# A graph layer on one core: the order of the end rewritten, and the row products done part by part

## The chip, the core and the metric

The kernel runs on one core of one Trainium2 chip. The core has five engines that run their own instruction streams beside each other: TensorE (PE; its weight loads are shown apart, as PEld), VectorE (DVE), ScalarE (ACT), GpSimd (POOL) and SyncE (SP). SP, ACT and POOL also issue DMA transfers. The metric is the device time of one execution in microseconds (us), smaller is better. It was 2201.93 us before the change, the median of 3 runs (2199.54 to 2204.43).

## The reference

There are N = 12500 nodes with 128 features and E = 212500 edges, sorted by destination, with 128 features and a weight each. The layer has 8 heads of 16 features. Cut to what matters:

```python
h = relu(layernorm(x))
q, v = h @ Wq.T + bq, h @ Wv.T + bv          # per node
k    = edge_attr @ Wk.T + bk                 # per edge
logits = sum16(q[src]*k), sum16(q[dst]*k), sum16(q[src]*q[dst])   # 3 x 8 per edge
score  = (softmax_by_dst(l0/4) + softmax_by_dst(l1/4) + softmax_by_dst(l2/4)) * weight**lam
out    = segment_sum(score[..., None] * v[dst], dst) @ Wo.T + bo
return x + leaky_relu(out, 0.1)
```

`softmax_by_dst` takes a maximum, an exponential and a sum over all edges with the same destination. As `v[dst]` is the same for all edges of a node, the sum over edges is a sum of scores per node and head, and the product with `v` is done once per node.

## The kernel before, in words

Edges are cut into blocks of 512 (`BE`), and the list into S = 5 parts of 83 blocks each. A turn t handles block t of all five parts; there are G = 83 full turns (0 to 82) and a short one, t = G = 83, which holds what is left over: the last 20 edges and the heads of the following parts. Below, g = 5t + s counts blocks.

In the main loop each block goes through PE, ACT and DVE. `turn` transposes the edge features, `project` makes k (`k_ps`), `spread_q` makes q of the destination (`qd_ps`), POOL gathers q of the sources (`gather`, line 702), and `logits` (lines 1250 to 1253, DVE) multiplies and sums by head. Per turn, with the five parts side by side in 120 rows (5 x 24 logits), there follow:

- `turn_logits` (PE, `l_ps`), `turn_head` (PE, `h_ps`) and `scan_here`, `scan_head`, `scan_on` (DVE, `u`, `u_head`, `head`): running maxima along the edges;
- `scan_back` (DVE, `m`): the same backwards, which gives each edge its node's maximum;
- `turn_max` (PE, `m_ps`), `powers` (DVE subtracts, ACT takes the exponential; tile `back`), `weigh_powers` (DVE, times the edge's weight);
- `show_ends` (PE `d_ps`, ACT; tile `sel`): a 0/1 matrix that says which of 42 (`W`) consecutive nodes an edge belongs to;
- `to_rows` (PE `w_ps`, line 1403; ACT copies to `rows`, line 1408): the sums per node, as products of `sel` and `back`;
- `put_rows` (SP, line 1419): five DMAs per turn that write each part's 42 rows to `sums[s]` in memory, at a node that is known only at run time. `fetch` loads these node numbers into registers (line 665).

Before the change `to_rows` multiplies three parts by three parts at once and keeps the diagonal blocks:

```python
trios = [(0, (0, 1, 2)), (S - 3, (1, 2))]      # 126 columns of sel by 144 of back, 2 x 4 products
```

Nodes are finished in units of 256, two units at a time (class `Nodes`): `load_sums`, `scores` (`scores_of`, lines 1112 to 1118: add, clamp, reciprocal, multiply, add, add), `turn` (PE and an ACT copy), `project_v`, `weigh` (DVE, line 1178), `turn`, `project_o` (PE, then a scaled ACT copy, line 1189), `add_x` (DVE, lines 1194 and 1195), `store` (SP). Most pairs do this inside the loop. What is left for the end is the last pair (`last_pair`, units 8 and 47) and `rest`: five groups of units, [18, 9], [10, 19], [28, 29], [38, 39] and [48]. Seven of these nine units lie across two parts, so a second transfer (issued by ACT, into `more`) and an add (line 1732) complete their sums. Each group of `rest` holds its product with Wv in a PSUM bank (`hold`).

The order on each engine is written out by hand: `pin` chains every instruction to the one pinned before it on the same engine, so an engine takes its instructions in the order of the source lines. [...] PSUM tiles made by `small` share three buffers. The end, from the line `leaving, last_pair = ...` on, is one such written order. The register load of line 665 was not pinned.

## Time and profile before

| | us |
|---|---|
| median of 3 runs | 2201.93 (2199.54 to 2204.43) |
| the profiled execution | 2203.34 |
| its span | 2201.5 |
| DVE busy | 2050.1 (93%) |
| PE busy | 1779.5 (81%) |
| POOL busy | 1586.5 (72%) |
| ACT busy | 1372.0 (62%) |
| last gather leaves POOL | 2131.2 |
| last `logits` of the loop on DVE ends | 2137.9 |

How to read the rows. A row of a timeline gives the start in us from the begin of the span, the busy time, the engine, the line, the operation, the tiles (written <- read), the shapes, how many instructions were merged (x16), and in brackets how long the engine stood before it and what released it. A row of the page gives a group's busy time and mean ns, then the idle time before its instructions. A row of waits gives the sum, the number of times and the longest. A row of windows gives the busy time of PE, PEld, DVE, ACT and POOL in that stretch, then the granted PE clock (1.00 is full) and the DMA share. One fp32 product of PE shows as two records, a transpose as one. Names with q (SPq, ACTq) are the engine's queue, here DMA issues and register loads.

### The profile page before, as it was taken

The numbers are of one execution on the slowest core, as the hardware profiler recorded it, in microseconds if no ns is written. First come the engines' busy times: TensorE is split into PE (matmuls) and PEld (weight loads), VectorE is DVE, ScalarE is ACT, GpSimd is POOL, SyncE is SP. The second block draws the span as 40 slices with busy tenths as digits, with TensorE's granted clock in tenths as the row PEclk, the third lists the DMA queues.
The fourth block names the chain that finished last, engine by engine and source line by source line (L and its number), as shares of the span: only waits on it lengthen the run. The fifth ranks groups of instructions, "written<-read, shape, count | busy, mean of one in ns | idle before, by whom it ended". The sixth has DMA issues, their size and how long they took to land.

```text
span 2201.5 us, 36690 instructions
## 1 busy us (share of the span) xinstructions
PE 1779.5 (81%) x10812; PEld 1418.5 (64%) x10812; DVE 2050.1 (93%) x2893; ACT 1372.0 (62%) x2555; POOL 1586.5 (72%) x1676
## 2 busy tenths in 40 slices
PE   4677888877887888888888888888888978888785
PEld 2565766666666666666766766766666767666664
DVE  6877999999999999999999999999999999999994
ACT  4777656665666566666656666666666656666671
POOL 7746777777777777777777777777777777777750
PEclk8788778787788778877878787787878787787887
DMA  8585456556646555655555565565555555555531
GB/s 227 168 252 159 145 150 181 158 162 177 169 148 189 165 161 154 187 162 164 157 169 154 144 186 149 156 171 151 151 167 162 154 170 155 150 171 158 156 99 58
DMA packets 373744, 355.66 MB, mean 162 GB/s; under 512 B 187698, under 2 KB 293437, under 8 KB 373327
## 3 DMA queue, kind: packets, MB, share of 16 engines
q1 hardware_dynamic: 304493, 237.91, 37.1%
q0 software_dynamic: 53184, 108.92, 17.8%
q10 hardware_dynamic: 15856, 6.39, 1.2%
q8 instruction: 87, 1.43, 0.3%
q14 instruction: 124, 1.02, 0.2%
HBM read 320.83 MB, written 32.17 MB: 160 GB/s over the span
## 4 chain that ended last, share of the span: by engine, by line
DVE 50%; PE 14%; DMA 11%; issue 4%; ACT 3%; POOL 1%; DVEq 1%; SPq 0%; ACTq 0%; POOLq 0%
DVE lT L1253 18%; DMA qq<-q_table,sources 11%; DVE prod L1250 7%; DVE prod L1252 7%; DVE prod L1251 7%; DVE m L1343 4%; PE k_ps L1231 4%; DVE l_ps L1313 3%; PE w_ps L1403 2%; PE eT_ps L1222 2%; DVE back L1363 1%; POOL qq L702 1%; PE m_ps L1355 1%; PE k_ps L1229 1%; DVE back L1375 1%
## 5 line engine op out<-in xcount | busy, mean ns | idle before, releaser
L702 POOL DMA_INDIRECT qq<-q_table,sources x1580 | 1498.2, 948 | 520.1 <-issue 219.1
L1253 DVE TENSOR_REDUCE lT<-prod 128x96 f32<-128x1536 f32 x415 | 727.4, 1753 | 14.3
L1231 PEld LDWEIGHTS k_ps<-wk,eT 128*128 128x128 f32 x3320 | 505.6, 233 | 201.2 <-issue 199.9
L1231 PE MATMUL k_ps<-wk,eT 128*128 128x128 f32 x3320 | 597.2, 335 | 0.7 <-ACT eT L1224 0.7
L1242 ACT COPY qd<-qd_ps 128x512 f32<-128x512 f32 x415 | 244.4, 589 | 138.7 <-DVE prod L1252 133.3
L1222 PE MATMUL eT_ps<-ident,ea 128*128 128x128 f32 x1660 | 310.3, 319 | 18.5 <-ACT eT L1224 16.1
L1364 ACT ACTIVATE back<-back 128x480 f32<-128x480 f32 x83 | 50.1, 604 | 416.8 <-DVE back L1363 416.8
L693 ACT ACTIVATE relb<-relb,before 126x512 bf16<-126x512 bf16 x415 | 303.4, 731 | 0.0
L1250 DVE TENSOR_TENSOR prod<-qq,qd_ps 128x512 f32<-128x512 f32 x412 | 279.0, 677 | 14.6 <-ACT qd L1242 9.1
L1239 PE MATMUL qd_ps<-win,oh 126*128 126x128 bf16 x1660 | 189.5, 245 | 124.2 <-DVE prod L1250 95.4
L1252 DVE TENSOR_TENSOR prod<-qd,k_ps 128x512 f32<-128x512 f32 x415 | 281.7, 679 | 0.0
L1251 DVE TENSOR_TENSOR prod<-qq,k_ps 128x512 f32<-128x512 f32 x412 | 279.7, 679 | 0.0
L1224 ACT COPY eT<-eT_ps 128x512 f32<-128x512 f32 x415 | 239.7, 578 | 62.6 <-PE eT_ps L1222 53.6
L1222 PEld LDWEIGHTS eT_ps<-ident,ea 128*128 128x128 f32 x1660 | 232.6, 165 | 60.0 <-ACT eT L1224 41.6
L694 ACT ACTIVATE oh<-relb 126x512 bf16<-126x512 bf16 x415 | 261.4, 630 | 13.2
L1239 PEld LDWEIGHTS <-oh 126*128 126x128 bf16 x1660 | 151.9, 112 | 148.2 <-issue 138.2
L1229 PE MATMUL k_ps<-b,ones 3*128 3x512 bf16 x415 | 186.7, 450 | 73.0 <-DVE prod L1252 70.9
L1403 PE MATMUL w_ps<-back,sel 128*126 128x144 f32 (+1 forms) x1344 | 212.6, 319 | 28.0 <-ACT sel L1393 12.6
L1403 PEld LDWEIGHTS w_ps<-back,sel 128*126 128x126 f32 (+1 forms) x1344 | 202.3, 219 | 34.4 <-ACT sel L1393 15.8
L1355 PE MATMUL m_ps<-ident,m 120*128 120x120 f32 x332 | 83.4, 400 | 85.4 <-DVE m L1343 80.8
L1355 PEld LDWEIGHTS m_ps<-ident,m 120*128 120x128 f32 x332 | 56.4, 217 | 104.1 <-DVE m L1343 67.4
L1343 DVE TENSOR_TENSOR_SCAN m<-far,head,l_ps 120x512 f32<-120x512 bf16 x81 | 102.9, 1271 | 0.0
(222 smaller groups left out, 1770.1 us busy)
## 6 DMA issues: line engine op xcount, KB each, us to landing
ea<-in_edge_attr_dram SPq DMA_DIRECT2D x83, 1280.0 KB
relb<-rel_d SPq DMA_DIRECT2D x83, 630.0 KB
qq<-q_table,sources POOLq DMA_INDIRECT x1580
win<-q_table SPq DMA_DIRECT2D x415, 31.5 KB
far<-far_d SPq DMA_DIRECT2D x84, 120.2 KB
q_table<-q SPq DMA_DIRECT2D x24, 384.0 KB
sums<-rows SPq DMA_DIRECT2D x412, 7.9 KB
q_table<-xq SPq DMA_DIRECT2D x24, 256.0 KB
```

Of the source, the lines that this page charges most:

```text
L693: pin(nc.scalar.activation(d, d, AF.Abs, bias=before[:K3]))
L694: pin(nc.scalar.activation(oh, d, AF.Relu, bias=1.0, scale=-1.0))
L702: rows = pin(nc.gpsimd.indirect_dma_start(out=qq[:, j, :], out_offset=None, in_=x if g < RAW else q_table, in_offset=bass.IndirectOffsetOn ...
L1222: pin(nc.tensor.transpose(eT_ps[:, j, :], eas[g // S][:, g % S, j * F:(j + 1) * F], ident))
L1231: pin(nc.tensor.matmul(k_ps[:, j, :], eTs[g][:, j, :], wk, start=False, stop=(j == JN - 1)))
L1239: pin(nc.tensor.matmul(qd_ps[:, j, :], ohs[g][:, j * P:(j + 1) * P], d["win"][:, s, :], start=(j == 0), stop=(j == JN - 1)))
L1242: pin(nc.scalar.copy(qds[g], qd_ps))
L1250: pin(nc.vector.tensor_mul(prod[:, :, 1, :], qqs[g], q_ps[g]))
L1251: pin(nc.vector.tensor_mul(prod[:, :, 0, :], qqs[g], ks[g]))
L1252: pin(nc.vector.tensor_mul(prod[:, :, 2, :], qds[g], ks[g]))
L1253: pin(nc.vector.tensor_reduce(lTs[t][:, :, s, :], prod.rearrange("p j i (h d) -> p j (i h) d", d=DIM), AX.X, ALU.add))
L1403: pin(nc.tensor.matmul(w_ps[:, i].rearrange("p s c -> p (s c)"), d["sel"][:n, j, lo:lo + 3, :].rearrange("p s w -> p (s w)"), d["back"][:n ...
```

## The change

Five things change.

1. **Row products by part.** `to_rows` makes one product per part and column group, 42 columns of `sel` by 48 of `back`: 20 products where there were 8. `w_ps` and `rows` have 42 rows of 5 x 48; `rows` has three buffers. This holds for all 84 turns. The tile `back` of the short turn becomes two tiles from the pool of x, in two halves, with two exponentials and two weighings.
2. **The order of the end.** `show_ends` of the turns G-1 and G, which stood in the last step of the loop, is spread over the end; `turn_logits(G-1)` comes first; scans, `turn_max`, `powers`, `weigh_powers`, `to_rows` and `put_rows` of the last three turns are interleaved turn by turn; the last pair's `scores` and `weigh` come after them.
3. **Two queues for the last rows.** The short turn's five row DMAs are issued by ACT. The node numbers of that turn are loaded into registers of SP and of ACT, and both loads are pinned at their place in the loop (turn G-2, step 3).
4. **Neighbouring units.** `rest` becomes [9, 10], [18, 19], [28, 29], [38, 39] and [48]; the sums of a group come with one transfer per part (`load_last`): five on SP, then four on ACT.
5. **Scores pair by pair.** Each group adds its second part (the first on DVE, the other three on POOL), computes its own scores, weighs, turns and projects (into the bank it held) before the next group begins; `add_x` and `store` follow two groups later.

```diff
-        _, base_v[t] = nc.values_load_multi_w_load_instructions(
-            places[0:1, t, 0:S], engines=[mybir.EngineType.SP], min_val=0, max_val=N - 1,
+        to = [mybir.EngineType.SP] if t < G else [mybir.EngineType.SP, mybir.EngineType.Activation]
+        loads, base_v[t] = nc.values_load_multi_w_load_instructions(
+            places[0:1, t, 0:S], engines=to, min_val=0, max_val=N - 1,
...
+        if t == G:
+            for inst in loads:
+                pin(inst)
...
+        def load_last(self, to, q, which):
+            of = [u for u in self.of if len(parts_of(u)) > which]
+            if of:
+                s, i = parts_of(of[0])[which], self.of.index(of[0])
...
+                pin(q.dma_start(
+                    to[:, 2 * i:2 * (i + len(of))].rearrange("p (u k) i c -> p u (k i c)", k=2),
+                    sums[s][of[0] * UN:(of[0] + len(of)) * UN].rearrange(
+                        "(u p k) i c -> p u (k i c)", p=P, k=2)))
...
-    rest = [Nodes(rest[i:i + 2]) for i in range(0, len(rest), 2)]
+    rest, left = [], sorted([u for _, u in todo] + [u for u in range(NU) if stored_at(u) is None])
+    while left:
+        n = 2 if len(left) > 1 and left[1] == left[0] + 1 else 1
+        rest.append(Nodes(left[:n]))
+        left = left[n:]
+    rest.sort(key=lambda of: -of.n)
...
-            w_ps = small([3 * W, 2, 3, 2 * H3], "w_ps")
-            for i, (lo, _) in enumerate(trios):
+            w_ps = small([W, S, 2 * H3], "w_ps")
+            for s in range(S):
                 for j in range(JN):
...
+                    pin(nc.tensor.matmul(w_ps[:, s, :], d["sel"][:n, j, s, :],
+                                         d["back"][j][:n, s].rearrange("p i c -> p (i c)"),
+                                         start=(s == 0 and j == 0), stop=(s == S - 1 and j == JN - 1)))
-            rows = work.tile([3 * W, 2, 3, 2 * H3], F32, name="rows")
+            rows = work.tile([W, S, 2 * H3], F32, name="rows", bufs=3)
...
-                    for i in (G - 2, G - 1, G):
-                        show_ends(i)
+                    show_ends(G - 2)
...
-        leaving.store()
-        put_rows(G - 3, range(1, S))
         turn_logits(G - 1)
-        last_pair.scores()
         last_pair.turn(small([P, JN, P], "node_ps"))
+        show_ends(G - 1)
+        leaving.store()
+        put_rows(G - 3, range(1, S))
         scan_on(G - 1)
-        hold(rest[0], "eT_ps")
-        last_pair.project_v(ps.tile([P, JN, F], F32, name="k_ps", bufs=2))
         scan_back(G - 2)
         turn_max(G - 2)
         scan_on(G)
         scan_back(G - 1)
+        powers(G - 2)
+        last_pair.project_v(ps.tile([P, JN, F], F32, name="k_ps", bufs=2))
+        scan_back(G)
         turn_max(G - 1)
-        scan_back(G)
+        weigh_powers(G - 2)
+        show_ends(G)
         turn_max(G)
-        for t in (G - 2, G - 1, G):
-            powers(t)
-        for t in (G - 2, G - 1, G):
-            weigh_powers(t)
+        powers(G - 1)
+        to_rows(G - 2)
+        put_rows(G - 2)
+        powers(G)
+        weigh_powers(G - 1)
+        to_rows(G - 1)
+        put_rows(G - 1)
+        weigh_powers(G)
+        to_rows(G)
+        put_rows(G, q=nc.scalar)
+        last_pair.scores()
         last_pair.weigh(last_pair.held)
-        for t in (G - 2, G - 1, G):
-            to_rows(t)
-            put_rows(t)
-        for r, of in enumerate(rest):
-            of.load_sums(ends_ab[:, r * JN:r * JN + of.n], of.more)
-        for r, name in ((1, "k_ps"), (2, "qd_ps"), (3, "qd_ps"), (4, "k_ps")):
-            hold(rest[r], name)
         last_pair.turn(small([P, JN, P], "node_ps"))
+        hold(rest[0], "eT_ps")
         last_pair.project_o(small([P, JN, F], "node_ps"))
+        for which, q in ((0, nc.sync), (1, nc.scalar)):
+            for r, of in enumerate(rest):
+                of.load_last(ends_ab[:, r * JN:r * JN + of.n] if which == 0 else of.more, q, which)
+        for of, name in zip(rest[1:], ("k_ps", "qd_ps", "qd_ps", "k_ps")):
+            hold(of, name)
         last_pair.add_x(nc.vector)
         last_pair.store()
-        ab = ends_ab[:, :sum(of.n for of in rest)]
+        score = scan.tile([P, len(rest) * JN, HEADS], F32, name="end_score", bufs=1)
         for r, of in enumerate(rest):
+            ab = ends_ab[:, r * JN:r * JN + of.n]
             if of.more is not None:
-                some = ends_ab[:, r * JN:r * JN + of.n]
-                pin(nc.vector.tensor_add(some, some, of.more))
-        score = scan.tile([P, len(rest) * JN, HEADS], F32, name="end_score", bufs=1)
-        scores_of(ab, score[:, :ab.shape[1]])
-        for r, of in enumerate(rest):
-            of.score = score[:, r * JN:(r + 1) * JN]
+                pin((nc.vector if r == 0 else nc.gpsimd).tensor_add(ab, ab, of.more))
         for r in range(len(rest) + 2):
             if r < len(rest):
-                rest[r].weigh(rest[r].held)
-            if 0 <= r - 1 < len(rest):
-                rest[r - 1].turn(small([P, JN, P], "node_ps"))
+                of = rest[r]
+                of.score = score[:, r * JN:(r + 1) * JN]
+                scores_of(ends_ab[:, r * JN:r * JN + of.n], of.score[:, :of.n])
+                of.weigh(of.held)
+                of.turn(small([P, JN, P], "node_ps"))
+                of.project_o(of.held)
             if 0 <= r - 2:
-                rest[r - 2].project_o(small([P, JN, F], "node_ps"))
                 rest[r - 2].add_x(nc.vector)
                 rest[r - 2].store()
```

58 lines of the change are left out of this document (27 added, 31 removed).

## The prediction

> **What bounds the kernel now.** I read the page first, then the waits and the timeline of the loop, then the timelines of the five engines and the chain of waits from 2131 us to the end. The page says that VectorE (DVE) is busy nearly always and GpSimd (POOL) issues one row gather after another; TensorE (PE) has room.
>
> ```profile
> span 2201.5 us, 36690 instructions
> PE 1779.5 (81%) x10812; PEld 1418.5 (64%) x10812; DVE 2050.1 (93%) x2893; ACT 1372.0 (62%) x2555; POOL 1586.5 (72%) x1676
> L702 POOL DMA_INDIRECT qq<-q_table,sources x1580 | 1498.2, 948 | 520.1 <-issue 219.1
> ```
>
> 1580 gathers at 0.948 us, with 0.3 us between (520.1 / 1580 = 0.33), are about 2020 us of issue in a row: a floor for the loop that no part of the change touches. DVE meets that floor only at the very end: the last gather leaves POOL at 2131.2 and its products start 3 us later, which is a landing (2.4 us, row below) and little more.
>
> ```profile
> 2130.28 0.95 POOL L702 DMA_INDIRECT qq<-q_table,sources  x1 [0.30 <-issue]
> 2134.21 0.68 DVE L1250 TENSOR_TENSOR prod<-qq,qd_ps 128x512 f32<-128x512 f32 x1
> DVE u_head L1321 <- PE h_ps L1281: 2.9, 2, 2.2
> 202.50 0.58 PE L1281 MATMUL h_ps<-ident,lT 16*120 16x16 f32 x4
> 203.12 0.35 DVE L1321 TENSOR_TENSOR_SCAN u_head<-far,carry,h_ps 120x64 f32<-120x64 bf16 x1 [0.70 <-PE h_ps L1281]
> 2116.13 0.40 PE L1281 MATMUL h_ps<-ident,lT 16*120 16x16 f32 x4
> 2118.92 0.35 DVE L1321 TENSOR_TENSOR_SCAN u_head<-far,carry,h_ps 120x64 f32<-120x64 bf16 x1
> ```
>
> These pairs (first and last of 81) show where PE stands nearest to DVE in a turn: `h_ps` follows the row products of `to_rows` on PE, and DVE's `u_head` needs it. I took the distance from the end of the one to the start of the other for all 81: it is 0.04 us in the first pair and 2.4 in the last; 2 are below 0.5 us, 6 below 1.0, 20 below 1.5, 30 below 2.0. What `to_rows` grows by eats from that.
>
> The end of the kernel is 64 us in which no engine is full. Rows of the timeline, of ACT's waits and of the chain, in order of time:
>
> ```profile
> 2134.44 3.01 PE L1403 MATMUL w_ps<-back,sel 128*126 128x144 f32 x16 [2.29 <-DVE back L1375]
> 2137.38 2.17 PE L1389 MATMUL d_ps<-shows,ends_t 21*128 21x420 bf16 x4
> 2141.24 1.11 PE L1273 MATMUL l_ps<-ident,lT 128*120 128x128 f32 x4
> 2142.38 1.28 DVE L1331 TENSOR_TENSOR_SCAN u<-far,u,l_ps 120x512 f32<-120x512 bf16 x1 [1.14 <-PE l_ps L1273]
> 2147.11 0.20 DVE L1348 TENSOR_TENSOR m_end<-head,l_end 120x64 f32<-120x64 f32 x1
> 2151.31 6.31 PE L1403 MATMUL w_ps<-back,sel 128*126 128x144 f32 x48 [1.19 <-DVE back L1375]
> ACT back L1368 <- PE w_ps L1403: 2.5, 1, 2.5
> ACT rows L1408 <- DMA sums<-rows: 2.2, 1, 2.2
> 2154.41 8.77 SPq L1419 DMA_DIRECT2D sums<-rows  x15
> 2159.53 1.34 SPq L665
> 2162.91 4.03 ACTq L1145 DMA_DIRECT2D qq<-sums  x7
> 2163.28 5.75 SPq L1143 DMA_DIRECT2D ends_ab<-sums  x9
> 2164.63 2.36 DMA qq<-sums
> ACT hT L1165 <- DMA qq<-sums: 8.4, 1, 8.4
> 2170.35 0.70 DVE L1194 TENSOR_TENSOR node_ps<-h,node_ps 128x512 f32<-128x512 f32 x1 [14.97 <-ACT h L1189]
> 2171.69 1.95 DVE L1732 TENSOR_TENSOR ends_ab<-ends_ab,qq 128x384 f32<-128x384 f32 x4
> 2179.40 0.69 DVE L1178 TENSOR_TENSOR qq<-eT_ps,end_score 128x512 f32<-128x512 f32 x1
> 2194.41 0.42 DVE L1195 TENSOR_TENSOR qq<-node_ps,qq 128x256 f32<-128x256 f32 x1
> ```
>
> To be seen: DVE stands 15 us before 2170.35, while SP puts out fifteen row blocks (with a register load of 1.34 us among them) and both queues issue sixteen loads; then 7.7 us (2171.69 to 2179.40) of sums and scores for all the last units before the first of them goes on.
>
> **The change, part by part.** I lay the new order along the clock with these durations. Turns are G-2 = 81, G-1 = 82, G = 83.
>
> *Before the scans.* Of three `show_ends` only that of 81 stays ahead of `turn_logits`: after `w_ps` (2137.5, taken as long as before, see below) two `d_ps` at 0.55 and `l_ps` at 1.1 end at 2139.7. The scan starts at 2139.75, not 2142.38: 2.6 earlier. The scores of the pair that DVE did in that gap move to where it waits for PE and ACT, at no cost as long as it does wait.
>
> *Scans to row products.* Six scans took 4.9 us (2142.38 to 2147.3); with the subtraction for 81 among them `weigh_powers(81)` ends at about 2146.2. But PE gets there later: behind the `m_ps` of 81 (2143.8) now stand `project_v` of the last pair, `m_ps` of 82, `show_ends(83)` and `m_ps` of 83.
>
> ```profile
> 2145.74 0.60 PE L1168 MATMUL k_ps<-b,ones 3*128 3x512 bf16 x1
> 2146.27 2.08 PE L1170 MATMUL k_ps<-wv,hT 128*128 128x128 f32 x8
> 2146.00:2149.00 3.00, 3.00 (x14) 2.73 (x14) 1.31 (x2) 0.00 (x0) 0.00 (x0) 0.50 0.00 0
> ```
>
> That is 2.5 + 0.9 + 1.1 + 0.4: the products of 81 start at 2148.45 (2151.31 before, 2.9 earlier). ACT must take the two new `d_ps` and the 0.9 us rectifier ahead of the exponential of 82; that one ends at about 2150, its weights at 2150.6, still before PE is through with 81. The window (PE, weight loads, DVE, ACT and POOL busy, then the granted clock) shows 0.50 although PE was busy all 3.00 us of it; I keep that. [...]
>
> *Row products by part.* 20 products of 42 columns by 48 in place of 8 of 126 by 144: 40 records for 16, in each of 84 turns.
>
> ```profile
> 2061.71 2.23 PE L1403 MATMUL w_ps<-back,sel 128*126 128x144 f32 x16 [1.23 <-ACT sel L1393]
> 2061.71 2.01 PEld L1403 LDWEIGHTS w_ps<-back,sel 128*126 128x126 f32 x16 [1.42 <-ACT sel L1393]
> L1281 PE MATMUL h_ps<-ident,lT x328: 202/205/278, 162.7 to 2116.3; 16*120 16x16 f32 x164
> ```
>
> No row has this shape. Low end: by streamed columns, 20 x 48 against 8 x 144, 0.83 of 2.23 = 1.9 us. The nearest small product is `h_ps`: four in 0.40 us, one 0.205, so (0.40 - 0.205) / 3 = 0.065 us a step; 40 steps are 2.6 + 0.2 = 2.8 us, 0.6 more than now. High end: nothing of the loading hidden, `h_ps`'s 0.065 plus a load at the 0.05 that 42 of 126 columns of a 0.13 us load (2.01 / 16) make, 0.1 us or more: 4.2 us, 2.0 more. I take 2.8, since `h_ps` loads 120 columns at that pace and these load 42. At the lowered clock 16 records cost 3.0 us (2134.44), and by columns 40 cost no more. In the loop +0.6 on PE meets the distances above: the sum of what lies below 0.6 us is about 1.1 us in all; DVE waits for the last gathers anyway, so I take +0.5 for the whole loop. ACT's copy of the rows shrinks a little (240 columns for 288), hidden.
>
> *Rows out.* Three products at 2.8 end at 2151.2, 2154.0 and 2156.8 (before: all at 2157.5). A third `rows` buffer and a `back` of its own for 83 remove the waits of 2.2 and 2.5 us in ACT's rows. SP puts 81 from 2151.7 and 82 from 2154.4 at 0.55 each, done by 2157.2. The register load leaves SP's end and runs in turn 81 on SP, and a second one on ACT: ACT is busy 62% of the span, so I take nothing; at worst the whole load (1.3 us). ACT puts 83 itself: five issues at 4.03 / 7 = 0.58, 2157.1 to 2160.0. SP's last put was issued at about 2162.9.
>
> *Loads.* 9 + 7 become 5 + 4 with the same bytes, as neighbouring units share a transfer. Behind ACT's puts stand the `hT` copy (0.6), `project_o` on PE (1.5 with its bias) and the scaled copy (0.6; rows in the next fence), and only then ACT's loads: the first is issued at 2162.9 and lands 2.36 later, at 2165.3. SP's loads wait for the landing of ACT's puts, issued from 2157.1 on, and land no later than ACT's. The first add ends at 2165.85. The adds of the other three pairs go to POOL, for which no row has a price; each has 2.7 us or more before DVE wants it, so nothing, up to about 2 us if one takes 4.
>
> *Scores pair by pair.*
>
> ```profile
> 2093.58 0.33 DVE L1112 TENSOR_TENSOR ab<-ab 128x192 f32<-128x192 f32 x1
> 2095.50 0.19 DVE L1118 TENSOR_TENSOR score<-score,ab 128x32 f32<-128x32 f32 x1
> 2169.72 0.60 ACT L1189 ACTIVATE h<-node_ps 128x512 f32<-128x512 f32 x1 [2.16 <-PE node_ps L1170]
> 2188.43 1.16 PE L1170 MATMUL node_ps<-wo,qq 128*128 128x128 f32 x8
> 2185.38 0.70 DVE L1194 TENSOR_TENSOR node_ps<-qq,node_ps 128x512 f32<-128x512 f32 x1 [4.10 <-ACT qq L1189]
> 2186.72 0.68 DVE L1178 TENSOR_TENSOR qq<-qd_ps,end_score 128x512 f32<-128x512 f32 x1
> ```
>
> One pair's scores are 2.1 us (2093.58 to 2095.69). The first `weigh` starts at 2168.0, not 2179.40: 11.4 earlier. From there DVE has 0.6 (weigh) + 3 x (2.1 + 0.6) + 1.85 (the half pair) + 4 x 1.33 (`add_x`) + 0.8 = 16.7 us, against 15.4 before (2179.40 to 2194.83), which had PE and ACT on its path (4.1 us of waiting in one place). Now a pair's turn, copy, product and scaled copy (0.5 + 0.6 + 1.5 + 0.6 at full clock, 4.1 at half) run beside the next pair's scores, so DVE sets the pace. DVE ends at 2184.7 instead of 2194.83: 10.1 earlier. The stores and closing waits behind it (6.7 us) stay.
>
> **Sum.** 10.1 less in the end, 0.5 more in the loop: 9.6 less. The profiled execution took 2203.34 us (span 2201.5, 1.84 around it), which gives 2193.7; it stands 1.4 above the median shown, 2201.93, from which it would be 2192.3. I say 2193.
>
> **The rivals.**
> - *The small products load in series* (slower). Price 0.1 us a record, 4.2 us per `to_rows`, 2.0 more: over the 81 distances the shortfall adds up to 20 us of DVE stalls in front of `u_head`, and three products in the end cost 4 more: -10 + 20 + 4 = +14, about 2216. It decides from about +1.6 a turn (0.09 a record), where the shortfall of 9 to 10 us and the end's 3 use up the gain. For it: `u_head` already waits twice. Against: 2.01 us of loads lie inside 2.23 us of products above, so loading is hidden today. [...]
> - *ACT becomes the queue that everything stands in* (no change). Its five puts, copy, scaled copy and four loads are one chain with PE in it. If the puts cost ACT 0.9 each, `project_o` meets the half clock (0.60 + 2.08 instead of 1.5) and the landing of the puts holds the loads, the first add comes 4 us later, and with the half clock in the last pairs (4.1 a pair instead of 2.7 on DVE) 2 to 3 more are lost: 2197 to 2201. For it: ACT's wait of 8.4 us on a load's landing. Against: it needs several rows at their worst.
> - *More than forecast.* The products at 1.9 and the full clock: 3 to 5 us lower, 2188.
>
> **How the numbers follow.** Forecast 0.57 (2189 to 2197.5), more than forecast 0.08, ACT's queue 0.13, serial loads 0.15, and 0.07 for another stall in the 84 changed turns, which DVE, tied with POOL at the end, would hand on in full. A measurement of this kernel tells about 0.2% (4.4 us) from no change. Faster 0.65, same 0.13, slower 0.22. The range goes from 2186 to 2210, taking in both bounds but the far end of the serial loads.
>
> **What would show it.** The scan of 82 starts near 2139.8; L1403 has 3360 records and a `to_rows` in the loop takes 2.6 to 2.9 us; the wait of `u_head` on `h_ps` stays below 5 us in total; ACT issues five puts near 2157 to 2160; reciprocals of 128x192 instead of one of 128x432; DVE's 15 us wait shrinks to below 8; the last add ends near 2185. Wrong if DVE's idle time in the loop grows by tens of us, or if the first add stands behind ACT's loads past 2169.

## The result, and the profile after

The changed kernel takes 2197.26 us (median of 8 runs, 2193.90 to 2202.43), the kernel before in the same comparison 2202.29 us (8 runs, 2199.32 to 2205.87). The ratio is 0.9979 with a 95% interval of 0.9969 to 0.9988: 5.0 us faster, where 9.3 were forecast. The direction was right, the size about half.

The profiled execution of the changed kernel took 2193.90 us, its span 2192.1 us, 9.4 us less than the span before. That pair of executions flatters the change. First the page of the changed kernel: its engines, and the group of the row products.

```profile
span 2192.1 us, 40695 instructions
PE 1770.3 (81%) x12828; PEld 1397.7 (64%) x12828; DVE 2053.7 (94%) x2915; ACT 1367.9 (62%) x2556; POOL 1588.5 (72%) x1679
L1422 PE MATMUL w_ps<-back,sel 128*42 128x48 f32 x3320 | 196.0, 230 | 28.2 <-ACT sel L1414 16.2
```

PE has 2016 records more and is busy 9 us less: the small products are cheap (196.0 us for these 3320 records, 210.4 for the 1328 that they replace). The reduction of `logits` opens and closes the loop on DVE. Its first and last row, in the timeline of the kernel before and then in that of the changed kernel:

```profile
137.69 1.75 DVE L1253 TENSOR_REDUCE lT<-prod 128x96 f32<-128x1536 f32 x1
...
2136.12 1.75 DVE L1253 TENSOR_REDUCE lT<-prod 128x96 f32<-128x1536 f32 x1
```

```profile
135.29 1.75 DVE L1266 TENSOR_REDUCE lT<-prod 128x96 f32<-128x1536 f32 x1
...
2133.40 1.75 DVE L1266 TENSOR_REDUCE lT<-prod 128x96 f32<-128x1536 f32 x1
```

Three stretches follow. Ahead of the loop 2.4 us were gained, where nothing was changed; the ten profiles of the table further down begin the loop anywhere from 134.0 to 140.6 us. The loop takes 1998.4 us before and 1998.1 after. From the last reduction to the end of the span it is 65.4 us before (2201.5 - 2136.12) and 58.7 after: 6.7 less, where the forecast has 10.1. Here is that end in the changed kernel, DVE first:

```profile
2136.85 1.28 DVE L1344 TENSOR_TENSOR_SCAN u<-far,u,l_ps 120x512 f32<-120x512 bf16 x1 [0.36 <-PE l_ps L1286]
...
2159.00 0.69 DVE L1203 TENSOR_TENSOR node_ps<-h,node_ps 128x512 f32<-128x512 f32 x1 [5.41 <-ACT h L1198]
...
2162.07 0.56 DVE L1753 TENSOR_TENSOR ends_ab<-ends_ab,qq 128x384 f32<-128x384 f32 x1 [1.66 <-DMA qq<-sums]
2162.66 0.36 DVE L1116 TENSOR_TENSOR ends_ab<-ends_ab 128x192 f32<-128x192 f32 x1
2163.06 0.96 DVE L1118 TENSOR_SCALAR ends_ab<-ends_ab 128x96 f32<-128x96 f32 x1
2164.05 0.75 DVE L1119 RECIPROCAL ends_ab<-ends_ab 128x96 f32<-128x96 f32 x1
2164.84 0.61 DVE L1120 TENSOR_TENSOR ends_ab<-ends_ab 128x96 f32<-128x96 f32 x1
2165.48 0.86 DVE L1121 TENSOR_TENSOR end_score<-ends_ab 128x32 f32<-128x32 f32 x1
...
2166.61 0.69 DVE L1187 TENSOR_TENSOR qq<-eT_ps,end_score 128x512 f32<-128x512 f32 x1
...
2167.60 0.21 DVE L1118 TENSOR_SCALAR ends_ab<-ends_ab 128x96 f32<-128x96 f32 x1
...
2183.41 0.42 DVE L1204 TENSOR_TENSOR qq<-k_ps,qq 128x256 f32<-128x256 f32 x1
```

POOL, PE, ACT with its queue, and SP's queue in the same stretch:

```profile
2162.95 0.99 POOL L1753 TENSOR_TENSOR ends_ab<-ends_ab,qq 128x384 f32<-128x384 f32 x1 [33.65 <-DMA out_dram<-x_in]
2164.34 1.96 POOL L1753 TENSOR_TENSOR ends_ab<-ends_ab,qq 128x384 f32<-128x384 f32 x2 [0.40 <-POOL ends_ab L1753]
```

```profile
2146.22 4.90 PE L1422 MATMUL w_ps<-back,sel 128*42 128x48 f32 x80
2151.05 1.89 PE L1422 MATMUL w_ps<-x_in,sel 16*42 16x48 f32 x40
2154.13 2.36 ACTq L1433 DMA_DIRECT2D sums<-rows  x5
2156.53 0.59 ACT L1174 COPY hT<-node_ps 128x512 f32<-128x512 f32 x1 [3.20 <-DMA sums<-rows]
2184.67 0.26 SPq L1212 DMA_DIRECT2D out_dram<-qq  x1
```

The one wait of 15.0 us on DVE is now two, 5.4 and 1.7 us. The first pair's scores take from 2162.66 to the `weigh` at 2166.61, 3.95 us, where one pair was reckoned at 2.1: the rows of lines 1118, 1120 and 1121 are two to five times as long as the same rows one pair later (line 1118: 0.96, then 0.21). And DVE is done at 2183.83, 8.3 us ahead of the end of the span, where this was 6.7 before.

### The profile page after: what moved, and what is told of

It is laid out like the page before. It is cut to its first block, busy times and chain, and to the rows that moved or that the text cites. A ratio compares the mean times of both kernels' runs of the same rounds, so it can differ in the third digit from the quotient of the medians.

```text
span 2192.1 us, 40695 instructions
## 1 busy us (share of the span) xinstructions
PE 1770.3 (81%) x12828; PEld 1397.7 (64%) x12828; DVE 2053.7 (94%) x2915; ACT 1367.9 (62%) x2556; POOL 1588.5 (72%) x1679
## 4 chain that ended last, share of the span: by engine, by line
DVE 39%; PE 19%; DMA 12%; issue 5%; ACT 5%; POOL 2%; DVEq 1%; SPq 0%; ACTq 0%; POOLq 0%
DVE lT L1266 13%; DMA qq<-q_table,sources 11%; DVE prod L1263 5%; PE k_ps L1244 5%; DVE prod L1265 5%; DVE prod L1264 5%; PE w_ps L1422 4%; DVE m L1356 4%; PE eT_ps L1235 3%; POOL qq L706 2%; DVE l_ps L1326 2%; PE k_ps L1242 1%; PE m_ps L1368 1%; PE qd_ps L1252 1%; DVE back L1377 1%
## 5 line engine op out<-in xcount | busy, mean ns | idle before, releaser
L1244 PEld LDWEIGHTS k_ps<-wk,eT 128*128 128x128 f32 x3320 | 499.9, 231 | 196.5 <-issue 195.3
L1244 PE MATMUL k_ps<-wk,eT 128*128 128x128 f32 x3320 | 590.6, 332 | 0.7 <-ACT eT L1237 0.7
L1378 ACT ACTIVATE back<-back 128x480 f32<-128x480 f32 x83 | 50.1, 604 | 411.3 <-DVE back L1377 405.9
L1422 PE MATMUL w_ps<-back,sel 128*42 128x48 f32 x3320 | 196.0, 230 | 28.2 <-ACT sel L1414 16.2
L1422 PEld LDWEIGHTS w_ps<-back,sel 128*42 128x42 f32 x3320 | 185.4, 140 | 43.7 <-ACT sel L1414 20.4
```

What stands on the lines that cost most here:

```text
L1244: pin(nc.tensor.matmul(k_ps[:, j, :], eTs[g][:, j, :], wk, start=False, stop=(j == JN - 1)))
L1422: pin(nc.tensor.matmul(w_ps[:, s, :], d["sel"][:n, j, s, :], d["back"][j][:n, s].rearrange("p i c -> p (i c)"), start=(s == 0 and j == 0), ...
```

## The experiments

The kernels ran in five series, each on one chip and timed against the kernel before on that chip (the expectations say "call" for a series). In the second and third series the kernel before took 2202 us, as above; in the first, fourth and fifth 2753, 2747 and 2720 us. The chips of the third and the fifth series carry the same number; if that names one chip, the longer time is no fixed property of it. What makes it is open. It decides one of the questions, so each run is named with its kind of series: "2202" or "2750".

To set the ends side by side, this table counts from the start of the last reduction, for the kernels in series of 2202, one profile each; the loop is the time from the start of the first reduction to the start of the last. "Threes" are the row products as before the change, "part" those of the change.

| kernel | products | loop | first add ends | first weigh | DVE ends | span ends | ratio to before |
|---|---|---|---|---|---|---|---|
| before | threes | 1998.4 | | 43.3 | 58.7 | 65.4 | 1 |
| changed | part | 1998.1 | 29.2 | 33.2 | 50.4 | 58.7 | 0.9979 |
| `after_2` (changed) | part | 1999.8 | 30.0 | 33.8 | 51.1 | 59.4 | 0.9980 |
| `trios_2` | threes | 1998.1 | 29.7 | 33.3 | 50.6 | 58.5 | 0.9976 |
| `parts_only` | part | 2002.5 | | 43.6 | 59.2 | 65.7 | 1.0009 |
| `batch_2` | part | 2000.1 | 29.3 | 38.3 | 57.3 | 64.5 | 1.0015 |
| `half_first` | part | 2001.3 | | 30.2 | 52.7 | 59.5 | 0.9984 |
| `split_store` | part | 2001.7 | 30.4 | 34.8 | 52.3 | 61.1 | 0.9982 |
| `puts_sp` | part | 2000.6 | 28.7 | 31.0 | 50.1 | 57.3 | 0.9970 |
| `best` | threes | 1997.5 | 30.8 | 33.0 | 53.0 | 60.8 | 0.9974 |

**The row products, alone and left out.** `trios` and `trios_2` are the changed kernel with the products of before; `parts_only` is the kernel before with the products of the change; `after_again`, `after_2` and `after_3` are the changed kernel itself; `threes_sp` also has SP put the last rows (below).

```diff
-            for s in range(S):
-                for j in range(JN):
-                    ... w_ps[:, s, :], d["sel"][:n, j, s, :], d["back"][j][:n, s]      # 42 x 48
+            for i, (lo, _) in enumerate(trios):
+                for j in range(JN):
+                    ... w_ps[:, i], d["sel"][:n, j, lo:lo + 3, :], d["back"][j][:n, lo:lo + 3]   # 126 x 144
```

> The changed kernel once more, for more rounds and a second trace. Theory: the end alone got shorter, by 6.7 us from the last reduction of the loop to the end of the span (66.0 to 59.3 when both are counted from the start of that reduction), and the loop stands still; the other 2.7 us between the two profiled executions lie ahead of the loop, where executions differ by themselves. Then the ratio is 0.9965 to 0.998 (4 to 7.5 us), and the second trace has 59 to 60 us from the last reduction to the end, wherever its loop begins. Rival: the row products by part cost the loop 1 to 2 us; then the time from the first to the last reduction, 1998.4 us before and 1998.1 in the first trace, is 1999.5 or more here.

> The row products are done three parts by three parts again, all else as changed. Theory (a product costs by its streamed columns): 2.1 to 2.2 us per turn at full clock instead of 1.9, in the end three of them in a row, so 0.7 to 1.5 us slower in all and the loop unchanged. Rival (40 records cost more, as I forecast): the end gets up to 2 us faster.

> The kernel before with the row products by part alone (each part its own product of 48 columns, 80 more PE instructions for a step of two halves and none of the work at the end rearranged). Theory of the work: PE streams fewer columns, so a step's row products fall from 2.12 to 2.23 us to about 1.9 us and the loop stays as it is or gains up to 10 us (0.4%); the end gains 1.4 to 2 us from products of a last step that take 6.7 us in place of 8.3. Theory of the supply: PE's instructions cost by their number wherever the chip hands them on slowly. Then on a chip where the kernel before takes about 2750 us this edit alone costs 30 to 40 us (1.1 to 1.5%), and on one where it takes about 2202 us it costs nothing in the loop (within 3 us).

> The changed kernel with the row products of before (three row places of one half to a product, 40 products of 144 and 96 columns a step in place of 80 of 48 columns), all else of the change kept. Theory of the work: 1.5 to 2.5 us slower than the changed kernel, as the three products of a last step take 8.3 us again in place of 6.7. Theory of the supply: on a chip where the kernel before takes about 2750 us it is again 0.2% faster than that one, with the changed kernel 1% slower; where the kernel before takes about 2202 us both are within 3 us of one another, 5 us faster than before.

> The changed kernel once more, beside the three others on the same chip. Theory of the work: 0.9979 of the kernel before on every chip. Theory of the supply: 0.998 where the kernel before takes about 2202 us, 1.011 where it takes about 2750 us, as in the first call.

> The changed kernel beside the three below on the same chip: 0.998 of the kernel before where that one takes about 2202 us. Its loop, from the start of the first reduction of the logits to the start of the last, takes 1999 to 2002.5 us, with 3 to 6 us of waits of u_head for h_ps (seven runs with the row products by part so far: mean 2000.6).

> The changed kernel with the row products in threes and the last step's row blocks put by SP, as both were before. If the products by part cost the loop 2.6 us (1998.0 us from the first reduction to the last with threes in three runs, 2000.6 by part in seven) and give back at most 1.5 us in the last turns, this is 1 to 2.5 us faster than the edit of the row blocks alone, which measured 0.9970 with a wide interval: 0.996 to 0.997, with 1997 to 1999 us from the first reduction to the last. If the difference of the loops was chance, it is 0.997 to 0.998 with 1999.5 us and more.

Some counts in these expectations are off: from the last reduction to the end it is 65.4 and 58.7 us, not 66.0 and 59.3, and a step has 8 products of 144 columns (16 records) in threes and 20 of 48 (40 records) by part, so that the part products add 24 records a step (2016 / 84).

Series of 2202: `parts_only` 1.0009 (1.0000 to 1.0018), `trios_2` 0.9976 (0.9967 to 0.9986), `after_2` 0.9980 (0.9971 to 0.9988). Series of 2750: `after_again` 1.0110 (1.0093 to 1.0126), `after_3` 1.0102 (1.0085 to 1.0119), but `trios` 0.9978 (0.9969 to 0.9987) and `threes_sp` 0.9969 (0.9958 to 0.9980). So the products by part give nothing anywhere, and where the kernel takes 2750 us they cost some 35 us and turn the gain into a loss of 1%. All of the measured gain is in the other edits. The theory of the supply is nearer in both kinds of series than that of the work, with one correction in the series of 2202: there the loop is not free of them.

In those series the three kernels with threes take 1998.0 us for the loop in the mean (1997.5 to 1998.4), the seven with part 2000.6 (1998.1 to 2002.5): 2.6 us more. `parts_only` against the kernel before agrees with 2.0 us (interval 0 to 4.0). Of the 2.6 us, 1.6 are seen in the waits of DVE for `h_ps` (4.2 us in the mean against 2.7). Here they are first in `trios_2`, then in `parts_only`, with one of these waits from the timeline of `parts_only`:

```profile
DVE u_head L1334 <- PE h_ps L1294: 2.2, 2, 1.5
```

```profile
DVE u_head L1321 <- PE h_ps L1281: 6.2, 7, 2.2
...
1164.22 3.42 PE L1401 MATMUL w_ps<-back,sel 128*42 128x48 f32 x40
...
1170.24 0.40 PE L1281 MATMUL h_ps<-ident,lT 16*120 16x16 f32 x4
1170.68 0.35 DVE L1321 TENSOR_TENSOR_SCAN u_head<-far,carry,h_ps 120x64 f32<-120x64 bf16 x1 [0.92 <-PE h_ps L1281]
```

Kernels with threes wait there twice, both times at the loop's start, those with part three to seven times. Each further wait follows a turn whose products took 3.42 us for the 40 records, which is their time in the changed kernel at a granted clock of 0.50 (at 1042.26); yet threes take 4.18 us at that clock in the kernel before (at 679.64) without such a wait. Why the part products leave `h_ps` later is not settled.

In the series of 2750 more can be seen. PE's waits, first in `after_3`, then in `threes_sp` of the same series, and a step's products in the timeline of `after_again`:

```profile
PE w_ps L1422 <- issue: 77.1, 116, 4.4
```

```profile
PE w_ps L1424 <- issue: 4.4, 4, 2.5
```

```profile
1523.40 2.47 PE L1422 MATMUL w_ps<-back,sel 128*42 128x48 f32 x29
1526.29 0.20 PE L1422 MATMUL w_ps<-back,sel 128*42 128x48 f32 x1 [0.42 <-issue]
1527.02 0.20 PE L1422 MATMUL w_ps<-back,sel 128*42 128x48 f32 x1 [0.53 <-issue]
1527.77 0.55 PE L1422 MATMUL w_ps<-back,sel 128*42 128x48 f32 x9 [0.56 <-issue]
```

"issue" is time in which PE waited for nothing that the profile shows. In a series of 2202 (`after_2`) the products have no such row in their list of waits at all. So I read the series of 2750 as one in which PE's instructions come in late, and a step of many short ones is torn apart: 77 us of such waits in 84 steps with part, 4 with threes. The profile shows the waits and not the supply itself, so the supply as their cause is argued, not shown; and of the 73 us of difference only some 35 show in the time. The chain of waits agrees, in `after_3` and then in the changed kernel's own profile:

```profile
PE 45%; issue 17%; DVE 15%; ACT 10%; another core or an unknown queue 7%; DMA 3%; SPq 1%; POOL 1%; DVEq 1%; ACTq 0%; POOLq 0%
```

```profile
DVE 39%; PE 19%; DMA 12%; issue 5%; ACT 5%; POOL 2%; DVEq 1%; SPq 0%; ACTq 0%; POOLq 0%
```

There PE and its instructions set the pace, here DVE does.

**Number or shape: threes cut by columns.** `threes_cut` is `trios` with each product cut in three, 126 columns of `sel` by 48 of `back`.

```diff
-   w_ps[:, i]        <- sel[lo:lo + 3] (126 columns) x back[lo:lo + 3] (144)
+   w_ps[:, i, k, :]  <- sel[lo:lo + 3] (126 columns) x back[lo + k] (48),  for k in 0, 1, 2
```

> The changed kernel with the row products of before cut into three by columns: the same 126 columns of weights against 48 columns of back, three times, so 24 products (48 records) a step, nearly as many as by part (20 and 40) with the width of before. If PE's instructions cost by their number where the kernel before takes about 2750 us, this costs there what the products by part cost or some 20% more: 1.010 to 1.013. If it was the narrow shape (42 columns of weights), it stays at 0.997 to 1.000 there. Where the kernel before takes about 2202 us, the number adds 8 records of 0.045 us to a step's products (2.2 to 2.6 us in place of 1.9) and the loop, from the first reduction to the last, takes 2000 to 2003 us as by part: 0.998 to 1.000.

Measured in a series of 2750: 3144.17 us, 1.1577 (1.1553 to 1.1600). Neither theory had this. A step in its timeline, and the window of its first piece (the stretch, its length, the busy time, the records, the granted clock, the DMA share and GB/s):

```profile
1519.23 2.20 PE L1425 MATMUL w_ps<-back,sel 128*126 128x48 f32 x17
1521.63 0.20 PE L1425 MATMUL w_ps<-back,sel 128*126 128x48 f32 x1 [0.20 <-issue]
1522.35 3.96 PE L1425 MATMUL w_ps<-back,sel 128*126 128x48 f32 x30 [0.52 <-issue]
...
1519.23:1521.43 2.20, 2.13 (x17) 1.00 0.20 48
```

17 records in 2.20 us at the full clock are 0.13 us each, though only 48 columns stream. At the same clock of 1.00 a record of the threes, 126 columns of weights and 144 streamed, takes 2.23 / 16 = 0.139, and one by part, 42 and 48, takes 1.90 / 40 = 0.047 (the median step of the changed kernel's loop). Among these three shapes the pace went with the columns of weights, and hardly with what streams through them. The rows made no such difference: the short turn's 40 records of 16 rows take 1.89 us, 40 of 128 rows 1.90, both at a clock of 1.00. The kernel thus had nearly three times the work on PE instead of the same work in more pieces: PE is busy 798 us with the row products, 286 in `threes_sp_store_2` of the same series. Of these 512 us, 424 show in the time, 5.0 us a turn; in a series of this kind PE has the largest share of the chain (45% in `after_3`). Number and shape are not told apart by it. It only shows that `issue` hits the quick records harder: 29.4 us of such waits over 3984 records of 0.13 us here, 77.1 us over 3320 records of 0.047 us in `after_3`.

**The three sums back on DVE.** `adds_dve` moves the sums that the change gave to POOL to DVE, each ahead of its own scores.

```diff
-                pin((nc.vector if r == 0 else nc.gpsimd).tensor_add(ab, ab, of.more))
+                pin(nc.vector.tensor_add(ab, ab, of.more))      # just ahead of scores_of
```

> The three adds of second parts that POOL does go to DVE, each just ahead of its own pair's scores. Theory (POOL's adds slow DVE beside them): the first pair's scores, 3.9 us in the changed kernel, fall back to 2.1, and the first product with v starts 1.8 us earlier; DVE pays 3 x 0.57 for the adds later, so the time is the same within 1 us. Rival (the landing loads slow DVE's scores): the first scores stay near 3.9 us and the kernel gets 1.7 us slower.

Measured in the first series: 1.0118 (1.0099 to 1.0136), beside 1.0110 of the changed kernel, so no difference that can be told. But the first pair's scores are quick again:

```profile
2758.97 0.36 DVE L1116 TENSOR_TENSOR ends_ab<-ends_ab 128x192 f32<-128x192 f32 x1
2759.36 0.21 DVE L1118 TENSOR_SCALAR ends_ab<-ends_ab 128x96 f32<-128x96 f32 x1
...
2761.14 0.69 DVE L1187 TENSOR_TENSOR qq<-eT_ps,end_score 128x512 f32<-128x512 f32 x1
```

2.17 us from line 1116 to the `weigh`, where the changed kernel took 3.95. The three sums cost DVE 0.55 us each, 1.65 in all, which is what the faster scores gave. In the changed kernel the slowed operations end with POOL's sums: line 1118 at 2164.02 and POOL's first sum at 2163.94; line 1120 at 2165.45 and the second at 2165.33 (each of the two merged sums takes 0.99); line 1121 at 2166.34 and the last at 2166.30. The reciprocal between them keeps its 0.75 us. By these ends, 0.04 to 0.12 us behind POOL's, I read it that in these three operations DVE does not run slower beside POOL but stands until POOL's sum is over. What holds it there, and why the reciprocal is not held, no run shows.

**All scores in one go.** `batch` and `batch_2` are the changed kernel with the scores of all last units after the four sums.

```diff
+        scores_of(ends_ab[:, :sum(of.n for of in rest)], score[:, :sum(of.n for of in rest)])
         for r in range(len(rest) + 2):
-                scores_of(ends_ab[:, r * JN:r * JN + of.n], of.score[:, :of.n])
```

> All adds first, then the scores of all nine units in one batch as before the change, then the pairs; all else as changed. Theory: the batch takes 5.2 us plus the wait for POOL's third add (some 4.3 us after the first load has landed), where the first pair's scores took 3.9; but the later pairs lose their own scores of 2.2 us each, so the pairs are paced by PE, ACT and DVE in turn (15.4 us before the change against 17.2). Together 2 to 5 us slower than the changed kernel. Rival (pair by pair wins nothing, since DVE does 8.5 us of scores in either form): within 1 us.

> The changed kernel with all scores of the last units in one go after all four sums, as before the change (one reciprocal of 432 elements, 2.85 us), neighbours still paired in the loads and turns. If the scores pair by pair are where the end's gain comes from, the first weigh starts 4 to 5 us later than in the changed kernel (38.1 us behind the start of the last reduction in the earlier run of this edit, 33.2 to 34.1 with the change), DVE waits for ACT's scaled copies again (1.6 to 3.5 us a pair), and most of the gain of 4 to 5 us goes: 0.9995 to 1.001 of the kernel before. If the gain comes from the scans and the queues, it stays within 1.5 us of the changed kernel: 0.998.

Measured: `batch` 1.0148 (1.0128 to 1.0168), 12 us more than the changed kernel of its series; `batch_2` 1.0015 (1.0007 to 1.0024), 8 us more than the changed kernel had in its comparison, both more than expected. The timeline of DVE in `batch_2`:

```profile
2169.37 0.56 DVE L1753 TENSOR_TENSOR ends_ab<-ends_ab,qq 128x384 f32<-128x384 f32 x1 [2.38 <-DMA out_dram<-x_in]
2173.26 1.06 DVE L1116 TENSOR_TENSOR ends_ab<-ends_ab 128x864 f32<-128x864 f32 x1 [3.34 <-POOL ends_ab L1753]
2174.78 2.85 DVE L1119 RECIPROCAL ends_ab<-ends_ab 128x432 f32<-128x432 f32 x1
...
2184.34 0.70 DVE L1203 TENSOR_TENSOR eT_ps<-qq,eT_ps 128x512 f32<-128x512 f32 x1 [3.46 <-ACT qq L1198]
```

The first `weigh` comes 4.5 to 5 us later and the waits for ACT's scaled copies are back (3.46, and 1.59, 1.85 and 2.19 behind it). The whole gain is gone and a little more: with one batch the earlier scans, the two queues and the paired loads bring DVE to a wait for POOL (3.34 us) and then to products as slow as at the half clock. From the first `weigh` to DVE's end it is 19.0 us here, 17.2 in the changed kernel and 15.4 before; ACT waits 2.1 to 2.2 us for the product with Wo of each of the four pairs here; in the changed kernel it waits 2.17 us for the first two, at a granted clock of 0.50, and 1.25 for the other two, at 1.00. Before the change the clock is 1.00 from 2188 to 2195. So `batch_2` is not the old end with new loads: POOL keeps its sums, and each pair is turned and projected before the next. It shows that this order gains only with scores pair by pair. How much they would carry with the sums on DVE, or with the pairs in the order of before, was not run; nor were the paired loads and the order of the scans taken out alone.

**The end behind DVE.** Three edits of the stores. `half_first` takes the single unit 48 first among the last groups:

```diff
-    rest.sort(key=lambda of: -of.n)
+    rest.sort(key=lambda of: of.n)
```

> The changed kernel with the group of one unit (48 columns of scores, 256 of values) taken first among the last groups, where the change takes it last. If the 1.6 us that the closing grew by (8.27 us from DVE's end to the span's end, 6.67 before) come from the last unit's store, whose 106 partitions land late, the closing falls by 1 to 2 us, and the first weigh comes 0.8 to 1 us sooner since its scores are half as wide (0.19 to 0.45 us an operation in place of 0.19 to 0.75): 1 to 3 us faster than the changed kernel. If the closing is the price of stores that stand in one queue whatever comes last, the end is within 0.5 us of the changed kernel's.

Measured 0.9984 (0.9976 to 0.9993), like the changed kernel. The closing falls to 6.9 us, but DVE ends 1.6 us later than in `after_2` beside it: the sums of all four pairs are now POOL's, with DVE behind each, and the last pair waits 1.99 us for ACT, which itself waits 2.17 us for PE, as long as for a product at the half clock. `split_store` cuts the last store (96 and 10 partitions):

```diff
-    ... out[u * UN:, :] <- y[:LAST, :]
+    for a, b in ((0, 96), (96, LAST)):  ... out[u * UN + 2 * a:u * UN + 2 * b, :] <- y[a:b, :]
```

> The changed kernel with the last store (106 rows of places, 106 KB) sent as two transfers, one of 96 and one of 10 partitions. If that store's own pace ends the kernel (after its issue it still moves for 4.5 us at 16 to 60 GB/s, while 128 KB of 128 partitions land in 2 us), the closing behind DVE's end falls from 8.3 to about 7 us, less the 0.5 to 1 us that a second issue costs: 0.5 to 1.5 us faster than the changed kernel. If the stores ahead of it in the queue set its end, nothing changes or it is 0.5 to 1 us slower.

Measured 0.9982 (0.9971 to 0.9992); the closing is 8.75 us. The odd shape of the store is not the cause. `store_act` lets ACT issue the last unit's store and the one ahead of it:

```diff
-    pin(nc.sync.dma_start(...))
+    q = nc.scalar if late and (i == 1 or u == NU - 1) else nc.sync
+    pin(q.dma_start(...))
```

> The changed kernel with the last unit's store and the one ahead of it issued by ACT and SP in turn. If the closing grew because SP's issues stand in line (the last one leaves 0.84 us behind DVE's end where it was 0.32 before), it falls from 8.3 us to 7.2 to 7.8. If the transfers themselves are slow, wherever they are issued, it stays at 8 us and more.

It ran in a series of 2750: 1.0114 (1.0096 to 1.0133), the changed kernel beside it 1.0102. Its rows on DVE and on ACT's queue:

```profile
2761.63 0.42 DVE L1204 TENSOR_TENSOR qq<-k_ps,qq 128x256 f32<-128x256 f32 x1
...
2762.09 0.29 ACTq L1213 DMA_DIRECT2D out_dram<-qq  x1
```

The store leaves 0.04 us behind DVE's end, 0.84 in the changed kernel (2183.83 to 2184.67), and the closing is 7.05 us. In the three kernels with the stores on two queues it is 6.7 to 7.1 us, in the twelve others that end with unit 48 and its whole store on SP, behind the loads of the change, 7.2 to 8.3. So SP's line of issues makes part of the growth. Against the scatter of the runs this is too little to time.

**The last rows by SP.** `puts_sp` gives the short turn's five row blocks back to SP and drops ACT's register load.

```diff
-        put_rows(G, q=nc.scalar)
+        put_rows(G)
-        to = [mybir.EngineType.SP] if t < G else [mybir.EngineType.SP, mybir.EngineType.Activation]
+        to = [mybir.EngineType.SP]
```

> The changed kernel with the last step's five row blocks put by SP again, not by ACT, and the second register load in the loop left out. If putting them on ACT is worth what the prediction reckoned (the puts end at 2160.0 in place of 2162.9), the first add comes 1 to 3 us later and the kernel is 1 to 3 us slower than the changed one. If ACT's own work behind its puts (the turn's copy, the scaled copy, four loads) was held by them, that starts 2.4 us sooner and the first add is no later: within 1 us of the changed kernel, or up to 1 us faster.

Measured 0.9970 (0.9958 to 0.9982). The first add ends 28.7 us behind the last reduction (29.2 and 30.0 with the change), so ACT's puts won nothing. The change's ACT row at 2156.53 shows why: the `hT` copy stands behind five issues of 2.36 us. In this kernel POOL's sums fall one pair later, and the slowed operation with them, again to the end of POOL's instruction (POOL, then DVE of `puts_sp`; the first of the two merged sums ends at 2170.62, the operation at 2170.69):

```profile
2167.17 0.99 POOL L1753 TENSOR_TENSOR ends_ab<-ends_ab,qq 128x384 f32<-128x384 f32 x1 [33.60 <-DMA qq<-sums]
2169.63 1.95 POOL L1753 TENSOR_TENSOR ends_ab<-ends_ab,qq 128x384 f32<-128x384 f32 x2 [1.47 <-DMA qq<-sums]
```

```profile
2166.84 0.21 DVE L1118 TENSOR_SCALAR ends_ab<-ends_ab 128x96 f32<-128x96 f32 x1
...
2169.75 0.94 DVE L1118 TENSOR_SCALAR ends_ab<-ends_ab 128x96 f32<-128x96 f32 x1
```

**Put together.** `best` is `trios` with the sums on DVE and the split store; `threes_sp_store` is `trios` with the rows put by SP and the stores on two queues.

> The changed kernel with three edits together: the row products in threes as before the change, the three sums that it gave to GpSimd on DVE (each 0.56 us, just ahead of its scores), and the last store in two. If the first pair's scores were slowed by GpSimd's sums (3.9 us in place of 2.1), DVE's three sums cost as much as that saves, so that part moves nothing (within 0.5 us). The loop loses the waits of 0.3 to 1.4 us in front of u_head (1 to 3 us), and the store gives 0.5 to 1.5 us: 0.9965 to 0.9975 of the kernel before where that one takes about 2202 us, 1 to 4 us faster than the changed kernel. Where the kernel before takes about 2750 us the products in threes alone are worth 30 us and more against the changed kernel.

> All three together: row products in threes, row blocks by SP, last stores on two queues. By the sums of the terms 0.9955 to 0.9968 of the kernel before, 3 to 5 us faster than the changed kernel; if queues make no difference to the stores, the same as the kernel without that edit within 0.7 us.

> Row products in threes, row blocks by SP, last stores on two queues, once more. Where the kernel before takes about 2202 us: by the terms 6.5 to 8 us under it (0.9963 to 0.9970), 2 to 3.5 us under the changed kernel; the closing behind DVE's end is 7 to 7.3 us. Where it takes about 2750 us: 0.9967 again.

`best` measured 0.9974 (0.9964 to 0.9985) in a series of 2202, no better than `trios_2`. `threes_sp_store` measured 0.9967 (0.9957 to 0.9978) and 0.9970 (0.9960 to 0.9981), both in series of 2750; in the first of these two the changed kernel stands at 1.0102, so it beats both kernels there. Whether it beats the changed kernel in a series of 2202 too was not seen; its parts came to 0.9970 and 0.9976 there, beside 0.9979 and 0.9980, with intervals that overlap.

## Why the prediction was right in direction and wrong in size

- *Before the scans*: right. The scan of 82 starts 3.45 us behind the last reduction, 6.26 before: 2.8 earlier, forecast 2.6.
- *Scans to row products*: nearly. The products of 81 start 12.8 us behind the last reduction, 15.2 before: 2.4 earlier, forecast 2.9. (The forecast's own terms, 4.9 us from 2143.8, end at 2148.7 and not 2148.45, which is 2.6 earlier.) They start at the half clock (granted 0.50 up to 2148.70), as taken; the full clock that the rival with more than forecast counts on came only behind that.
- *Row products by part*, their price: I took 2.8 us a step by the pitch of `h_ps`. It is 1.9 us, the low end, and with `threes_cut` beside it the pace goes with the columns of weights (0.13 us a record for 126, 0.047 for 42). I had the right number from streamed columns, and for the wrong reason: streaming a third of the columns changes a record from 0.139 to 0.13 us. Nor is the 3.0 us at 2134.44 a price at the low clock: the granted clock is 0.89 up to 2136.00 and 0.50 after it. Wholly at the granted clock of 0.50, 16 records in threes take 4.18 us (679.64 in the kernel before), 40 by part 3.42 (1042.26 in the changed one). In the end this made the three products 6.7 us, not the 8.4 of the forecast, and nothing came of it: `trios_2` has its first add 0.5 us later than the changed kernel, `after_2` 0.8 later.
- *Row products by part*, the loop: wrong by 2.1 us in the series of 2202 (+2.6 against +0.5) and without measure in those of 2750 (+35). I looked for the cost in PE's work per step, and that fell (2.23 to 1.90 us); in the series of 2750 the cost came with PE's waits ahead of its instructions, and in those of 2202 it is seen in part in the waits for `h_ps` and otherwise open. The rival with serial loads fails too, its 0.1 us a record being 0.047 at the full clock and 0.086 (3.42 / 40) at half. The 7% for "another stall in the 84 changed turns" were all I had for what happened in three series of five.
- *Rows out* and *Loads*: the first add ends 29.2 us behind the last reduction; the forecast (2165.85 less 2136.12) is 29.7. Right in sum, though ACT's puts hold its own copy, as the rival of ACT's queue said at a smaller price.
- *Loads*, the sums on POOL: here the forecast fails first. "Nothing, up to about 2 us" looked at POOL's own time. What it costs is DVE's time: 1.8 us of the first pair's scores.
- *Scores pair by pair*: the mechanism is right, DVE sets the pace of the last pairs. The first `weigh` comes 10.1 us earlier (43.3 to 33.2) where 11.4 was forecast, 1.3 less; POOL takes 1.8 of it and the earlier add gives 0.5 back. The 10.1 are not the scores' alone: the first add ends at 29.2 where it ended at some 36.1 before (a quarter of the row at 2171.69), 6.9 earlier, and from there to the `weigh` it is 4.0 us where it was 7.2. From there DVE takes 17.2 us, forecast 16.7: 0.5 more.
- "The stores and closing waits behind it (6.7 us) stay": wrong by 1.6 us. The last three `add_x` end within 2.1 us of one another, before within 3.2, so the last stores come closer together. The last issue leaves 0.84 us behind DVE's end, before 0.32, which is 0.5 of it, and `store_act` takes that away; the other 1.1 us come after that issue, and their cause is open.

The sum again with these: 10.1 - 1.3 - 0.5 - 1.6 = 6.7 us in the end, the measured 65.4 - 58.7; less 2.6 in the loop, 4.1 us. Measured are 5.0, and by the interval of the ratio 2.6 to 6.8. So three steps of the prediction failed, each a term put too low: the row products by part in the loop (+0.5 forecast, +2.6 seen), the sums on POOL (nothing forecast, 1.8 us of DVE's time) and the closing ("stay" forecast, +1.6). The end as a whole misses by 3.4 us, the loop by 2.1, the largest single term. That the profiled pair differs by 9.4 us, close to the forecast, is luck: 2.4 of them lie ahead of the loop, and this pair does not show the loop's 2.6.

## What to carry to other kernels

Work moved to GpSimd was not free beside VectorE's work here, though GpSimd was idle (1.8 us of VectorE's time for three sums of 0.98): look at what VectorE does during those very microseconds, and give GpSimd its instructions where VectorE waits. When a chain is pulled tight, what used to stand between its last steps goes too (the last three `add_x` ended within 2.1 us in place of 3.2, and the closing grew from 6.7 to 8.3), so the stores behind it have to be reckoned anew and not carried over. And an edit that lowers an engine's busy time by more and shorter instructions should be timed on more than one occasion, since the same edit cost 2 to 3 us on one occasion and some 35 on another.

## What the hardware showed that I had not expected

- A DVE operation of 0.19 to 0.26 us beside a GpSimd sum of 0.98 us took 0.61 to 0.96 us and ended 0.04 to 0.12 us behind it (profiles of the changed kernel and of `puts_sp`); a reciprocal among them was not touched.
- The pace of short fp32 products at the full clock followed the columns of weights: 0.047 us a record for 42 at 48 streamed, 0.13 for 126 at 48, 0.139 for 126 at 144.
- The same kernel takes 2202 us in some series and 2720 to 2753 in others, with the same durations on DVE (the reduction has 1.75 us in both), but with waits on PE for nothing that the profile shows (77.1 us ahead of the row products in `after_3`, none in `after_2`) and waits on "another core or an unknown queue" (7% of the chain in `after_3`). 2016 more records on PE cost some 35 us there and 2 to 3 us here. The cause is open.
- The granted clock of PE came back in the middle of the last products, shown by windows of the changed kernel (length, busy time, records, clock, DMA share, GB/s):

```profile
2140.00:2143.00 3.00, 3.00 (x12) 0.50 0.00 1
2143.00:2146.00 3.00, 2.74 (x13) 0.50 0.00 0
2146.22:2148.70 2.48, 2.48 (x32) 0.50 0.03 7
2148.70:2151.05 2.35, 2.35 (x52) 0.93 0.02 3
```

  It was still half after 5.2 us of work without a gap (from 2139.83 to 2145.06 in PE's timeline), and full 3.7 us after the next piece of work had begun (2145.32; the last line's 0.93 puts the return 0.33 us into that stretch). Before the change it stayed half through 8.0 us without a gap (2140.39 to 2148.35, windows of the kernel before). So the length of a stretch of work alone did not tell when the clock came back: 5.2 and 8.0 us did not bring it, 3.7 us did. What brings it back is not shown.
